# One pool of x tiles for two layers, and the last stage's first blocks in another order

## The chip, the core and the metric

The kernel runs on one core of a Trainium2 chip. A core has five engines that run side by side, each through its own list of instructions in order: TensorE (PE; its weight loads are listed apart as PEld), VectorE (DVE), ScalarE (ACT), GpSimd (POOL) and SyncE (SP), which here only issues transfers. ScalarE and GpSimd can issue transfers too. An instruction waits for semaphores that others raise, and all that is behind it on its engine waits with it. The metric is the device time of one execution in microseconds; the median of three runs of the kernel before is 3335.99 us (3325.55 to 3337.98).

## What is computed

Four layers follow one another on an image of 256 x 256 points with 128 channels. Each normalises its input over groups of four channels and the whole image, and adds its own output to it. The first two are attention along rows and a product of triangles; they are left as they are. The change lies in the third and fourth:

```python
def _L2_conv_ref(z, ...):
    zn = _layernorm(z, ln_in_w, ln_in_b)
    a = jax.nn.sigmoid(zn @ Wga + bga) * (zn @ Wla + bla)
    b = jax.nn.sigmoid(zn @ Wgb + bgb) * (zn @ Wlb + blb)
    k = jnp.einsum('bimc,bmjc->bijc', a, b)
    return jax.nn.sigmoid(zn @ Wgo + bgo) * (_layernorm(k, ...) @ Wlo + blo)

def _L3_conv_ref(x, w1, b1, w2, b2):
    t = relu(c1(x))                      # 3 x 3 taps, 128 channels to 1
    y = jnp.concatenate([x[:, :1], x[:, 1:] + t[:, :-1]], axis=1)
    u = relu(c1(y))
    z_main = u + jnp.roll(y, 1, axis=1)
    z = jnp.concatenate([z_main[:, :H - 2], u[:, H - 1:H] + y[:, H - 2:H - 1], y[:, H - 1:H]], axis=1)
    v = relu(c2(z))                      # 128 x 128 product at each point
    p = jnp.concatenate([z[:, :, :1], z[:, :, 1:] + v[:, :, :-1]], axis=2)
    r = relu(c2(p))
    q_main = r + jnp.roll(p, 1, axis=2)
    return ...                           # q_main with its last two columns put right

x = x + _L2_conv_ref(_gn(x), ...)        # gives x3
x = x + _L3_conv_ref(_gn(x), ...)        # gives the output
```

`t` and `u` are single-channel images, so the shifts by one row and one column are done on small data; their sum, one number per point called `e` below, is added to all channels.

## The kernel before

Channels lie on the 128 partitions, and the 65,536 points are cut into 32 strips of 2048 points (8 rows), 1 MB each. Between stages the data lie in DRAM: `x2T` is the input of the third layer, `x3T` of the fourth. Tiles come from pools in SBUF that are opened and closed with their stage; a pool's place is used again by the next one, and a tile's place by a later tile of the same pool, after a wait for the earlier use. In most stages the program's order is written out by hand, one list for all engines.

The third layer has three stages. **Stage 5** (L1101 to L1235) loads x2T by strips (pool `x5`, seven tiles) and makes a and b. **Stage 6** (L1260 to L1299) multiplies them channel by channel and stores k; near its end it loads the first three strips of x2T again (`load7x`, pool `x7`). **Stage 7** (L1303 to L1407), the x3 stage, goes through the strips: GpSimd spreads a row of factors (L1329), TensorE makes the gate product and the output product (L1335), VectorE scales, adds biases and multiplies (L1345, L1324, L1391), GpSimd adds the result to x in place (L1404), ScalarE sums x and its square for the next normalisation (L1349, L1350), and SP stores x to x3T (L1356) and loads the strip five ahead. For the last strip VectorE does the addition in halves (L1397) and its halves are stored apart (L1401). Seven tiles hold x, three in `x7` and four in the stage's own pool.

From the sums come mean and deviation of each group (L1414 to L1420; `r3`), and from them the tap weights `w1f` (L1424) and constants.

**Stage 9** (L1451 to L1750) is the fourth layer. Its steps, by the names used in the prediction:

- `load9` loads a strip of x3T (L1462, nine tiles).
- `taps`: TensorE makes nine tap values for each point (L1468), ScalarE copies them (L1472, into one of two buffers `p9_st`), and SP stores them to a padded image sD in DRAM (L1477, four stores a strip; strip 0 also needs the last two rows, `xe`).
- `load_block` reads the taps of 16 rows (two strips) shifted into place (L1487); VectorE sums them (`sum_taps`, L1509, L1510); ScalarE applies relu (`relu_t`, L1515); GpSimd masks the image's edge and multiplies by the taps' weights (`shift_t`, L1519, L1522); t goes to DRAM (`keep_t`, L1527) and comes back one row lower (`load_t`, L1531); VectorE sums (`image_u`, L1536), ScalarE applies relu (`relu_u`, L1540), GpSimd adds u and t (`image_e`, L1545), and e goes to DRAM (`keep_e`, L1551). This is the image chain of one block.
- `load_e` reads e back as one row for each of the two strips (L1564, 8 KB each), and `spread_e` spreads a row over the partitions on GpSimd (L1572).
- `start_z`: ScalarE normalises x into PSUM, shifted by a row (L1580). `finish_z`: VectorE adds the spread e and gives z (L1595).
- `p_half` and `q_half`: TensorE's products (L1601) with VectorE's max and add (L1609, L1623, L1626); `residual` is GpSimd's addition (L1615); L1702, L1706 and L1750 are ScalarE's small preparations of p and q; `emit` transposes (L1638), copies (L1639) and stores the output (L1640).

The tap results, the started z and the transposed outputs share two PSUM buffers.

Before the loop over strips stands a prologue (L1644 to L1694): xe and four strips are loaded, taps of strips 0 and 1 made, blocks -1 (one row) and 0 taken through the image chain, and strips 2 to 7 prepared. In the loop (L1695 to L1750) the first two passes take blocks 1 and 2 through the whole chain inside one pass; from pass 2 on the chain of a block is laid over two passes, and ScalarE issues the loads of e's rows:

```python
            if s > 3 and s % 2 == 0 and b <= NB:
                load_e(b - 1, nc.scalar)
            if s < NR:
                p_half(s, 0)
                p_half(s, 1)
                del xs[s]
            if s < 2:
                begin_image(s + 1)
            if s + 1 < NR:
                finish_z(s + 1)
            if s < 2:
                end_image(s + 1)
```

Of the kernel before, what the change touches and what calls it, by code (L numbers as in the profile page):

```python
# [9 lines left out]
F32 = mybir.dt.float32  # L10
# [22 lines left out]
def kernel(ctx: ExitStack, tc: tile.TileContext, a: dict, out: bass.AP):  # L33
# [1061 lines left out]

    rs2_scope = ExitStack()
# [4 lines left out]
    with tc.tile_pool(name="x5", bufs=7) as x5_pool, tc.tile_pool(name="p5", bufs=2) as sb, tc.tile_pool(  # L1101
# [6 lines left out]
        def load5(s):  # L1108
            if s < NSC:
                xs[s] = x5_pool.tile([P, SC], F32, name="p5_x")  # L1110
                (nc.gpsimd if s < KB else nc.sync).dma_start(xs[s], x2T[:, s * SC : (s + 1) * SC])
# [127 lines left out]
    x7_pool = rs2_scope.enter_context(tc.tile_pool(name="x7", bufs=3))  # L1239
# [15 lines left out]
    def load7x(s, pool, bufs):  # L1255
        if s < NSC:
            xs7[s] = pool.tile([P, SC], F32, name="p7_x", bufs=bufs)
            nc.sync.dma_start(xs7[s], x2T[:, s * SC : (s + 1) * SC])

    with tc.tile_pool(name="p6", bufs=3) as sb, tc.tile_pool(name="p6ps", bufs=3, space=PSUM) as ps:  # L1260
        nc.vector.memset(k1, 0.0)
        nc.gpsimd.memset(k2, 0.0)  # L1262
        with tc.manual_schedule():
# [18 lines left out]
            for c in range(D):  # L1282
# [11 lines left out]
                if c % 4 == 3:  # L1294
# [3 lines left out]
                    if q >= D // 4 - 3:  # L1298
                        load7x(q - (D // 4 - 3), x7_pool, 3)  # L1299

    g1 = const.tile([P, NSC + 1], F32, name="g1")  # L1303
    g2 = const.tile([P, NSC + 1], F32, name="g2")
    with tc.tile_pool(name="p7", bufs=2) as sb, tc.tile_pool(name="p7psX", bufs=2, space=PSUM) as psX, tc.tile_pool(
# [46 lines left out]
        def finish7(s):  # L1352
            x = xs7.pop(s)
            sums7(x, junk, s)
            del gts[s]
            nc.sync.dma_start(x3T[:, s * SC : (s + 1) * SC], x)  # L1356

        load7k(0)
        load7x(3, sb, 4)
# [13 lines left out]
        load7x(4, sb, 4)  # L1373
# [9 lines left out]
        for s in range(NSC):  # L1383
# [3 lines left out]
            for h in range(2):  # L1387
# [3 lines left out]
                nc.vector.scalar_tensor_tensor(gts[s][:, hs], pl, b2w[:, 5:6], gts[s][:, hs], ALU.add, ALU.mult)  # L1391
# [4 lines left out]
                if last:  # L1396
                    nc.vector.tensor_tensor(xs7[s][:, hs], xs7[s][:, hs], gts[s][:, hs], ALU.add)  # L1397
                    if h == 0:
                        finish7(s - 1)
                    sums7(xs7[s][:, hs], junk[:, hs], s + h)  # L1400
                    nc.sync.dma_start(x3T[:, s * SC + h * H2 : s * SC + (h + 1) * H2], xs7[s][:, hs])  # L1401
            del ks[s]
            if not last:
                nc.gpsimd.tensor_tensor(xs7[s], xs7[s], gts[s], ALU.add)  # L1404
                if s:
                    finish7(s - 1)
            load7x(s + 5, *((x7_pool, 3) if (s + 5) % 7 < 3 else (sb, 4)))  # L1407
# [36 lines left out]
    R = 8  # L1444
    NR = N // R
    H = R // 2
    BR = 16
    NB = N // BR
    BW = NP // 8
    LEAD = 6  # L1450
    with tc.tile_pool(name="p9", bufs=2) as sb, tc.tile_pool(name="p9psM", bufs=2, space=PSUM) as psM, tc.tile_pool(  # L1451
        name="p9psX", bufs=2, space=PSUM
    ) as psX, tc.manual_schedule():
        x3r = x3T.rearrange("d (h w) -> d h w", w=N)
        xs, zs, pbs, qs, blocks = {}, {}, {}, {}, {}
# [3 lines left out]
        def load9(s):  # L1459
            if s < NR:  # L1460
                xs[s] = sb.tile([P, R, N], F32, name="p9_x", bufs=9)
                nc.sync.dma_start(xs[s], x3r[:, s * R : (s + 1) * R, :])  # L1462

        def taps(x, h0, n):
# [6 lines left out]
            st = sb.tile([P, 2, N], F32, name="p9_st")  # L1471
# [3 lines left out]
            for c in range(n):  # L1475
                at = 16 + (h0 + 2 * c + 1) * NP
                nc.sync.dma_start(  # L1477
# [4 lines left out]
        def load_taps(St, row, up, width, at, lo=0):  # L1482
# [4 lines left out]
            nc.sync.dma_start(  # L1487
# [6 lines left out]
        def load_block(b):  # L1494
            St = sb.tile([P, TAPS, 2 * BW + 8], F32, name="p9_S")
            load_taps(St, b * BR, 1, BW + 8, BW)
# [436 lines left out]
```

## Time and profile before

| | us |
|---|---|
| median of three runs (range) | 3335.99 (3325.55 to 3337.98) |
| the profiled execution | 3336.53 |
| its span | 3333.7 |
| TensorE busy in the span | 3044.9 (91%) |
| VectorE | 2241.9 (67%) |
| ScalarE | 2037.7 (61%) |
| GpSimd | 1769.6 (53%) |
| mean DMA rate | 225 GB/s |
| strip loop of stage 7 and its head, from 2645 | to about 2905 |
| mean and deviation known (`r3`) | 2920.8 |
| first finished z of stage 9 begins | 2951.9 |
| last output stored, end of the span | 3333.7 |

Times in the profile count from the start of the span. A line of the timeline gives the start, the duration, the engine, the line of the program, the operation, what it writes and reads, how many were merged into the line, and in brackets how long the engine stood idle before and what ended that. "ACTq", "SPq" are the engines' instruction queues, where issued transfers show. A line of the table by stretches gives the stretch, its length, busy time and number of instructions of the five rows PE, PEld, DVE, ACT and POOL, the granted TensorE clock as a share of full speed, the mean busy share of the 16 DMA engines, and GB/s. A profile is one execution; the end of a matmul is modelled.

### The profile page before, as it was taken

The numbers are of one execution on the slowest core, as the hardware profiler recorded it, in microseconds if no ns is written. First come the engines' busy times: TensorE is split into PE (matmuls) and PEld (weight loads), VectorE is DVE, ScalarE is ACT, GpSimd is POOL, SyncE is SP. The second block draws the span as 40 slices with busy tenths as digits, with TensorE's granted clock in tenths as the row PEclk, the third lists the DMA queues.
The fourth block names the chain that finished last, engine by engine and source line by source line (L and its number), as shares of the span: only waits on it lengthen the run. The fifth ranks groups of instructions, "written<-read, shape, count | busy, mean of one in ns | idle before, by whom it ended". The sixth has DMA issues, their size and how long they took to land. (4 is left out here: it accounts for less than half of the span.)

```text
span 3333.7 us, 51741 instructions
## 1 busy us (share of the span) xinstructions
PE 3044.9 (91%) x19780; PEld 1631.0 (49%) x19780; DVE 2241.9 (67%) x2532; ACT 2037.7 (61%) x2274; POOL 1769.6 (53%) x1012
## 2 busy tenths in 40 slices
PE   5678999999999999977897999999999999839988
PEld 4525555555555555532532344444799733314444
DVE  5626888888888888873555454454455688837866
ACT  3576777777777777744476544443444477726766
POOL 4055777777777777750286000000455588727866
PEclk7799999999999999989897999999999999969999
DMA  9982333333333333349599576775899899847764
GB/s 359 355 320 93 121 108 119 109 121 111 111 120 108 117 109 122 110 172 399 170 365 403 199 309 229 281 289 190 330 351 351 325 379 385 336 149 217 228 190 134
DMA packets 295170, 749.44 MB, mean 225 GB/s; under 512 B 71399, under 2 KB 142425, under 8 KB 245737
## 3 DMA queue, kind: packets, MB, share of 16 engines
q1 hardware_dynamic: 285671, 734.83, 61.1%
q0 software_dynamic: 8544, 9.99, 0.9%
q8 instruction: 158, 2.59, 0.3%
q10 hardware_dynamic: 704, 1.26, 0.1%
q14 instruction: 93, 0.76, 0.1%
HBM read 458.34 MB, written 287.64 MB: 224 GB/s over the span
## 5 line engine op out<-in xcount | busy, mean ns | idle before, releaser
L565 DVE TENSOR_TENSOR p_e<-p_S,triT 128x1024 f32<-128x1024 f32 x512 | 609.4, 1212 | 144.3 <-PE p_S L555 144.3
L575 POOL TENSOR_TENSOR p_es<-p_e 128x1024 f32<-128x1024 f32 x256 | 603.2, 2367 | 125.8 <-issue 65.1
L573 ACT ACTIVATE p_e<-p_e,mbT 128x1024 f32<-128x1024 f32 x512 | 552.0, 1138 | 61.4 <-DVE p_e L565 61.3
L1172 PE MATMUL p_pm<-p_zn,wf 128*128 128x512 f32 x1040 | 449.0, 593 | 2.5 <-ACT p_a L1207 1.9
L540 PE MATMUL p_mm<-p_xn,w 128*128 128x512 f32 x768 | 405.3, 611 | 0.3 <-DVE p_v L535 0.3
L1172 PEld LDWEIGHTS p_pm<-p_zn,wf 128*128 128x128 f32 x1040 | 196.7, 190 | 254.8 <-issue 248.1
L555 PE MATMUL p_S<-p_q,p_k 32*128 32x256 f32 x4096 | 295.4, 400 | 3.5 <-DVE p_e L565 3.3
L1262 POOL MEMSET k<- 128x512 f32 x1 | 0.5, 520 | 506.5 <-DVE p_zn L1165 506.5
L555 PEld LDWEIGHTS p_S<-p_q,p_k 32*128 32x128 f32 x4096 | 185.9, 184 | 159.5 <-PE p_mm L531 91.7
L514 POOL TENSOR_TENSOR p_xn<-p_xn,p_rs 128x1024 f32<-128x1024 f32 x63 | 151.2, 2400 | 205.7 <-DMA p_rb<-rzD 125.9
L1891 PE MATMUL tp_z<-p_B,tp_at 128*128 128x256 f32 x1024 | 249.3, 386 | 0.7 <-DMA p_B<-bD 0.5
L588 PE MATMUL p_o<-p_e,p_v 128*32 128x256 f32 x4096 | 248.6, 383 | 0.0
L1293 POOL TENSOR_TENSOR k<-k,p_sq 128x512 f32<-128x512 f32 x128 | 163.0, 1273 | 158.1 <-ACT p_sq L1291 158.1
L1891 PEld LDWEIGHTS tp_z<-p_B,tp_at 128*128 128x128 f32 x1024 | 184.5, 190 | 22.4 <-DVE tp_at L1882 1.5
L540 PEld LDWEIGHTS p_mm<-p_xn,w 128*128 128x128 f32 x768 | 126.0, 190 | 104.6 <-issue 88.6
L588 PEld LDWEIGHTS p_o<-p_e,p_v 128*32 128x32 f32 x4096 | 120.3, 110 | 110.3 <-ACT p_g L546 41.5
L1292 DVE TENSOR_TENSOR k<-tp_z,k 128x512 f32<-128x512 f32 x128 | 88.5, 691 | 125.7 <-ACT p_sq L1291 125.7
L1615 POOL TENSOR_TENSOR p_q<-p_q,p_pb 128x2024 f32<-128x2024 f32 x32 | 144.3, 4510 | 52.4 <-ACT p_q L1706 44.0
L1289 ACT COPY p_K<-tp_z 128x512 f32<-128x512 f32 x128 | 74.9, 585 | 156.5 <-PE tp_z L1891 156.5
L546 ACT ACTIVATE p_g<-p_mm,bgh 128x512 f32<-128x512 f32 x128 | 88.0, 687 | 131.4 <-PE p_mm L540 131.3
L544 ACT ACTIVATE p_k<-p_mm,cqkg 128x512 f32<-128x512 f32 x128 | 88.0, 687 | 125.2 <-PE p_mm L540 124.9
L531 PEld LDWEIGHTS p_mm<-w,p_xn 128*128 128x128 f32 x1024 | 134.4, 191 | 61.1 <-issue 60.4
(379 smaller groups left out, 6040.5 us busy)
## 6 DMA issues: line engine op xcount, KB each, us to landing
p_x<-x2T SPq DMA_DIRECT2D x60, 1024.0 KB
x<-x1T SPq DMA_DIRECT2D x51, 1024.0 KB
p_x<-in_x_dram SPq DMA_DIRECT2D x32, 1024.0 KB
p_x<-xT SPq DMA_DIRECT2D x64, 512.0 KB
x2T<-x SPq DMA_DIRECT2D x32, 1024.0 KB
aD<-p_a SPq DMA_DIRECT2D x32, 1024.0 KB
bD<-p_b SPq DMA_DIRECT2D x32, 1024.0 KB
p_A<-aD SPq DMA_DIRECT2D x32, 1024.0 KB
```

Of the source, the lines that this page charges most:

```text
L514: nc.gpsimd.tensor_tensor(xn, xn, groups[g]["rs"], ALU.mult)
L531: nc.tensor.matmul(pm[:, k * D : (k + 1) * D], lhsT=t["xn"][:, b * P : (b + 1) * P], rhs=wf[:, 2 * D : 3 * D], start=True, stop=True,)
L540: nc.tensor.matmul(pm, lhsT=w, rhs=t["xn"][:, cs_], start=True, stop=True)
L555: nc.tensor.matmul(Ss[h // 2][:, h % 2, u, :], lhsT=t["k"][hp, r * N + u * P : r * N + (u + 1) * P], rhs=t["q"][hp, r * N : (r + 1) * N], ...
L565: nc.vector.tensor_tensor(e[:, :, 2 * p : 2 * p + 2, :].rearrange("p u h n -> p h u n"), Ss[p], triT[:, 2 * p : 2 * p + 2, :, :], ALU.add,)
L573: nc.scalar.activation(e[:, u, :, :], e[:, u, :, :], AF.Exp, bias=mbT[:, u, i : i + 1])
L575: nc.gpsimd.tensor_tensor(es, e[:, 0, :, :], e[:, 1, :, :], ALU.add)
L588: nc.tensor.matmul(t["o"][hp, r % 2, :], lhsT=t["v"][:, r * 2 + u, hp], rhs=e[:, u, h, :], start=(u == 0), stop=(u == 1),)
L1172: nc.tensor.matmul(pm[:, c, :], lhsT=wf2[:, i, :], rhs=zns[s][:, k * CK : (k + 1) * CK], start=True, stop=True)
L1293: nc.gpsimd.tensor_tensor(k2, k2, sq, ALU.add)
L1615: nc.gpsimd.tensor_tensor(q[:, :, 1 : N - 2], q[:, :, 1 : N - 2], pb[:, :, 0 : N - 3], ALU.add)
L1891: nc.tensor.matmul(pz[:, t, :], lhsT=at[:, u, t * P : (t + 1) * P], rhs=Bc[:, u, :], start=(u == 0), stop=(u == 1))
```

## The change

Five things are done.

1. The seven x tiles become one pool `x57` opened before stage 5 and closed at the end. Stages 5, 6 and 7 take their x tiles from it, and stage 9 takes seven of its nine; two more lie in its own pool.
2. In stage 7, `load7x(s + 5)` is followed, when x2T has run out (strips 27 to 31), by `load9(0)` to `load9(4)`. The last two rows `xe` are read from the last strip's tile instead of being loaded.
3. Stage 7's last two strips: GpSimd's addition for strip 30 and its sums come in halves; for strip 31 VectorE writes the scaled product back to PSUM, adds x from there, and takes the sums with four `bn_stats` and a `bn_aggr` instead of ScalarE's four passes.
4. The prologue is put into another order: taps of strips 2 and 3 are made ahead of the image chain and stored by ScalarE, which also issues the loads of block 1; the chains of blocks 0 and 1 are interleaved; strip 5 is loaded by GpSimd, whose memset also clears the first block; strips 6 and 7 are loaded at its end. `p9_st` has three buffers. The edge masks `inside` are made between stages 6 and 7. Passes 0 and 1 of the loop are now like the others.
5. `load_e` in the loop is issued by SP, right after that pass's x load, and in each even pass from 2.

```diff
+    x_scope = ExitStack()
+    x_pool = x_scope.enter_context(tc.tile_pool(name="x57", bufs=7))
...
-                xs[s] = x5_pool.tile([P, SC], F32, name="p5_x")
+                xs[s] = x_pool.tile([P, SC], F32, name="p5_x", tag="x")
...
-    def load7x(s, pool, bufs):
+    def load7x(s):
         if s < NSC:
-            xs7[s] = pool.tile([P, SC], F32, name="p7_x", bufs=bufs)
+            xs7[s] = x_pool.tile([P, SC], F32, name="p7_x", tag="x")
...
+    inside = const.tile([P, BW + 8], F32, name="inside")
+    nc.vector.memset(inside, 1.0)
...
+    def load9(s, own=None, queue=nc.sync):
+        if s < NR:
+            if s % 9 < 7:
+                xs9[s] = x_pool.tile([P, R, N], F32, name="p9_x", tag="x")
+            else:
+                xs9[s] = own.tile([P, R, N], F32, name="p9_x")
+            queue.dma_start(xs9[s], x3r[:, s * R : (s + 1) * R, :])
...
         def finish7(s):
             x = xs7.pop(s)
-            sums7(x, junk, s)
+            if s < NSC - 2:
+                sums7(x, junk, s)
+            else:
+                for h in range(2):
+                    hs = slice(h * H2, (h + 1) * H2)
+                    sums7(x[:, hs], junk[:, hs], s + h)
...
+        def stats7():
+            nc.vector.bn_aggr(mv7[:, 0:2], st7.rearrange("p n s -> p (n s)"))
+            nc.vector.tensor_tensor(mv7[:, 2:3], mv7[:, 0:1], m2, ALU.subtract)
+            nc.vector.tensor_scalar(g1[:, NSC:], mv7[:, 2:3], float(SC), None, ALU.mult)
+            nc.vector.scalar_tensor_tensor(mv7[:, 3:4], mv7[:, 2:3], mv7[:, 2:3], mv7[:, 1:2], ALU.mult, ALU.add)
+            nc.vector.tensor_scalar(g2[:, NSC:], mv7[:, 3:4], float(SC), None, ALU.mult)
...
-                nc.vector.scalar_tensor_tensor(gts[s][:, hs], pl, b2w[:, 5:6], gts[s][:, hs], ALU.add, ALU.mult)
+                nc.vector.scalar_tensor_tensor(
+                    pl if last else gts[s][:, hs], pl, b2w[:, 5:6], gts[s][:, hs], ALU.add, ALU.mult
+                )
...
                 if last:
-                    nc.vector.tensor_tensor(xs7[s][:, hs], xs7[s][:, hs], gts[s][:, hs], ALU.add)
+                    nc.vector.tensor_tensor(xs7[s][:, hs], pl, xs7[s][:, hs], ALU.add)
                     if h == 0:
                         finish7(s - 1)
-                    sums7(xs7[s][:, hs], junk[:, hs], s + h)
+                    for c in range(2):
+                        k = 2 * h + c
+                        nc.vector.bn_stats(st7[:, k, :], xs7[s][:, k * CK : (k + 1) * CK])
...
+            elif s == NSC - 2:
+                for h in range(2):
+                    hs = slice(h * H2, (h + 1) * H2)
+                    nc.gpsimd.tensor_tensor(xs7[s][:, hs], xs7[s][:, hs], gts[s][:, hs], ALU.add)
...
-            load7x(s + 5, *((x7_pool, 3) if (s + 5) % 7 < 3 else (sb, 4)))
+            load7x(s + 5) if s + 5 < NSC else load9(s + 5 - NSC)
...
-            st = sb.tile([P, 2, N], F32, name="p9_st")
+            st = sb.tile([P, 2, N], F32, name="p9_st", bufs=3)
...
-        xe = sb.tile([P, 2, N], F32, name="p9_xe", bufs=1)
-        nc.sync.dma_start(xe, x3r[:, N - 2 : N, :])
-        for s in range(4):
-            load9(s)
+        xe = xs7[NSC - 1].rearrange("p (h w) -> p h w", w=N)[:, R - 2 : R, :]
         S0 = sb.tile([P, TAPS, 2 * BW + 8], F32, name="p9_S")
-        nc.vector.memset(S0, 0.0)
+        nc.gpsimd.memset(S0, 0.0)
+        load9(5, sb, nc.gpsimd)
...
         taps(xe, N - 2, 1)
         for s in range(2):
             taps(xs[s], s * R, 4)
-        start_z(0)
         load_taps(S0, N - 1, 1, BW, BW + 4, P - 8)
         blocks[-1] = dict(St=S0)
         load_block(0)
...
+        for s in range(2, 4):
+            taps(xs[s], s * R, 4, nc.scalar)
+        for b in (-1, 0):
             sum_taps(b)
             relu_t(b)
             shift_t(b)
-            keep_t(b)
-            load_t(b)
...
+            if b < 0:
+                nc.sync.dma_start(image_rows(tD, 0, 1), blocks.pop(b)["t"][P - 8 : P, 4 : 4 + BW])
+        keep_t(0)
+        load_t(0)
+        image_u(0)
+        load_block(1, nc.scalar)
+        relu_u(0)
+        for s in range(4, 6):
             taps(xs[s], s * R, 4)
-        load_block(1)
-        for s in range(4, 8):
-            load9(s)
+        start_z(0)
+        image_e(0)
+        keep_e(0)
+        load_e(0)
+        sum_taps(1)
+        relu_t(1)
+        shift_t(1)
+        keep_t(1)
+        load_t(1)
         spread_e(0)
         finish_z(0)
+        image_u(1)
+        relu_u(1)
+        image_e(1)
+        keep_e(1)
+        load_e(1)
         spread_e(1)
+        load_block(2)
+        load9(6, sb)
+        load9(7, sb)
         for s in range(NR + 2):
             b = s // 2 + 2
-            load9(s + 8)
-            if s > 1 and s % 2 == 1 and b < NB:
+            load9(s + 8, sb)
+            if s > 1 and s % 2 == 0 and b <= NB:
+                load_e(b - 1)
+            if s % 2 == 1 and b < NB:
                 load_t(b)
...
-            if s > 3 and s % 2 == 0 and b <= NB:
-                load_e(b - 1, nc.scalar)
...
-            if s < 2:
-                begin_image(s + 1)
             if s + 1 < NR:
                 finish_z(s + 1)
-            if s < 2:
-                end_image(s + 1)
...
-            if s > 1 and s + LEAD < NR:
+            if s + LEAD < NR:
                 taps(xs[s + LEAD], (s + LEAD) * R, 4)
-            if s > 1 and s % 2 == 1 and b + 1 < NB:
+            if s % 2 == 1 and b + 1 < NB:
                 load_block(b + 1)
```

## The prediction

> **What bounds the kernel.** I read the busy shares by stage first, to see where engines are idle; then the timeline of the end of the x3 stage and the start of the last one; then the waits and timeline of the last stage's loop. The kernel takes 3336.53 us in the profiled execution, 3333.7 of it span. The table by stretches (us; busy time of each engine with its instructions; TensorE clock; DMA share; GB/s):
>
> ```profile
> 2645.00:2905.00 260.00, 254.94 (x742) 98.88 (x742) 227.10 (x188) 188.62 (x180) 206.88 (x61) 0.99 0.96 373
> 2905.00:2922.00 17.00, 3.17 (x16) 1.66 (x15) 9.32 (x21) 12.33 (x16) 3.16 (x1) 0.63 0.35 142
> 2922.00:2952.00 30.00, 5.39 (x18) 0.61 (x18) 4.13 (x9) 5.62 (x9) 4.71 (x6) 0.56 0.48 167
> 2952.00:3005.00 53.00, 30.39 (x88) 9.77 (x88) 20.93 (x23) 19.75 (x26) 19.32 (x16) 0.72 0.45 143
> 3005.00:3290.00 285.00, 264.66 (x1040) 130.46 (x1040) 219.45 (x251) 199.96 (x258) 219.56 (x172) 0.97 0.70 202
> ```
>
> The x3 stage is full (TensorE 255 of 260 us). Then come about 100 us (2905 to 3005) in which no engine is full: a serial chain. The loop after it is nearly, not quite, full. The change touches exactly these two; nothing else in it is on a path. The chain, from the timeline:
>
> ```profile
> 2905.86 3.38 DVE L1397 TENSOR_TENSOR p_x<-p_x,gate 128x1024 f32<-128x1024 f32 x1
> ...
> 2917.40 0.19 DVE L1415 TENSOR_REDUCE d<-g 128x1 f32<-128x33 f32 x1 [1.09 <-ACT p_junk L1350]
> ...
> 2933.97 0.69 ACT L1472 ACTIVATE p_st<-p_pp,s 128x512 f32<-128x512 f32 x1 [4.93 <-DMA sD<-p_st]
> ...
> 2940.55 0.81 DVE L1509 TENSOR_REDUCE p_acc<-p_S 128x41 f32<-128x369 f32 x1 [0.31 <-DMA p_S<-sD]
> ...
> 2951.85 2.36 DVE L1595 TENSOR_TENSOR p_z<-p_zp,p_eb 128x1024 f32<-128x1024 f32 x2 [8.35 <-POOL p_eb L1572]
> 2964.92 2.35 DVE L1595 TENSOR_TENSOR p_z<-p_zp,p_eb 128x1024 f32<-128x1024 f32 x2
> ```
>
> See how long it takes from the last sums (2917.4) to the first block's tap sums (2940.6) and to the first finished z (2951.9). I call the start of the VectorE add of strip s z(s): z(1) is 2964.92, z(2) 2992.23, z(3) 3004.76, and z(5) 3023.64. From there z of an even strip to the next odd one always takes 9.77 us, in which TensorE is busy all the time; odd to even takes 9.5 to 16:
>
> ```profile
> 3045.18:3059.33 14.15, 11.67 (x42) 5.38 (x40) 8.74 (x11) 9.30 (x11) 9.04 (x8) 0.88 0.86 242
> 3099.88:3109.65 9.77, 9.77 (x42) 4.79 (x40) 7.86 (x10) 7.71 (x11) 7.66 (x6) 1.00 0.52 155
> 3109.65:3120.56 10.91, 9.98 (x42) 4.79 (x40) 8.79 (x11) 7.76 (x11) 9.09 (x8) 1.00 1.04 298
> ```
>
> From z(5) to z(27) (3023.64 to 3266.56) are 11 pairs in 242.9 us, 22.08 each; at two times 9.77 they would take 214.9. So 28.0 us are lost here, and the timeline says to what:
>
> ```profile
> 3049.36 1.25 ACTq L1564 DMA_DIRECT2D p_er<-eD  x2
> 3051.13 0.69 ACT L1472 ACTIVATE p_st<-p_pp,s 128x512 f32<-128x512 f32 x1 [4.39 <-DMA p_er<-eD]
> ...
> 3112.22 1.66 ACTq L1564 DMA_DIRECT2D p_er<-eD  x2
> 3114.06 0.69 ACT L1472 ACTIVATE p_st<-p_pp,s 128x512 f32<-128x512 f32 x1 [2.84 <-PE p_pt L1638]
> ...
> 3055.38 2.30 POOL L1572 PARTITION_BROADCAST p_eb<-p_er  x1 [3.67 <-DMA p_er<-eD]
> 3116.45 2.30 POOL L1572 PARTITION_BROADCAST p_eb<-p_er  x1 [0.26 <-DMA p_er<-eD]
> ```
>
> ScalarE itself issues the loads of e's rows: it stands until the store of e has landed, and then for 1.25 to 2 us of issue; the tap copy and the output copies behind it free the PSUM buffers that TensorE needs.
>
> **The end of the x3 stage.** VectorE's first add of the last strip (3.38 us, waiting out GpSimd's add; the second took 1.23) now reads PSUM: 1.22, as L1324 took beside a busy GpSimd. The last strip's sums leave ScalarE (4.9 us, 2912.45 to 2917.37) for VectorE: four statistics at 0.685 (L648). GpSimd's add of strip 30 goes in halves and ends near 2907.1 instead of 2908.16, since its first half needn't wait for the second gate. VectorE from 2905.83: 1.22 + 1.37 + 1.28 + 1.22 + 1.37, and five small operations of 0.2, an estimate from the 0.16 to 0.22 of L1416 to L204: 2913.3, then both reductions, so L1415 starts at 2913.55. ScalarE ends its sums at 2911.65 (2902.52 + 4.2 + 4.9) and loads the square root's table in the gap. **-3.9 us.**
>
> **To the first tap sums.** After the statistics, before waits for xe (2923.69 where the weights were ready at 2921.7: 2.0), for the x strips (0.79 + 0.61), and ScalarE's third copy waits from about 2930.5 to 2933.97 for a tap buffer (3.5), whose small store lay behind 4 MB of x loads. With x and xe in SBUF and a third buffer all go: 3.9 + 2.0 + 1.4 + 3.5 = **10.8, taken as 10.5**: 2930.0 instead of 2940.55. The x loads moved up take the slots of strips already stored; the loads of x2T and k that they follow run out there, so their cover is the fading traffic of strips 27 to 31 (stores 1 MB per 5.7 us). Without cover they cost 4 MB at 420 GB/s, 9.5 us.
>
> **To z(0).** The chain t, u, e took 11.3 us. Its SP steps now stand behind eight tap stores of strips 4 and 5 (2.5 us), and relu_u behind two issues of block 1 on ScalarE (1.0); some of it lies beside the wait for t. I get 12.5: 2942.5, **-9.3**. Unknown from the trace: whether ScalarE's tap stores of strips 2 and 3 must wait for block 0's load to finish reading. If so ScalarE stands 4 us at 2926, of which 2.9 reach z(0). Ends 0 and 2.9; the nearest row, SP's tap store at 3008.62 that starts 0.75 us after its copy ended, after a block load, says rather yes.
>
> **To z(3).** Before, strips 1 and 2 each paid a whole image chain in the loop (z(1) to z(2) 27.3 us). Now block 1's chain lies beside block 0's: z(1) is 6.7 later (VectorE's two products, then GpSimd's spread 2.3), 2949.2. For z(2), block 2's row e isn't needed (block 1 holds strips 2 and 3), but ScalarE's tap copy of strip 6 stands ahead of strip 2's start, and strip 6 is only loaded after z(0), near 2949.7. Before, four such loads issued at 2961.48 gave their first strip at 2968.5, 7 us later. So taps at 2956.7, copy 2959.3, start and q 4.7, products: z(2) 2964, z(3) 2973.3. That is -28 and -31.4. From z(3) to z(5) took 18.9, and will take 19.5 to 21. With half the unknown wait and a little more, **-28 at z(5)**; ends -19 (strip 6 late by another load time, the wait in full) and -34. The masks' VectorE operations (0.9 us, 2921.8 to 2922.7) now stand ahead of the chain of k between stages: **+0.9**. The shared pool moves addresses in earlier stages; their first loads wait for stores anyway, cost 0, ends -2 and +3.
>
> **The loop.** Taking the issue from ScalarE gives at most 28.0. What is late next: the row must land before GpSimd's spread (2.3), which must end before z(even). [...]moved to SP's queue, the 8 KB rows stand behind the 1 MB x load just issued there. The row that shows it: the tap store issued at 2926.36 behind x loads landed about 2933.97, 7.6 us, where with a free queue the rows at 2947.32 were used at 2949.52. In the pair at 3109.65, SP issues block, output and x load from 3108.16 to 3112.64, 2.44 MB; 1.25 MB of it had moved by 3114 (the stretches of 1 us from 3109 sum to that), so the rest at 310 GB/s drains near 3117.8, against 3116.45 by the separate queue. [...]row at 3118, spread to 3120.3, z 10.6 after z(odd), and with t's store, 5 us in flight behind the next megabyte, pairs of 20.4 to 21.3. Without it (landing 0.9 after issue): 19.54. I take 20.7[...]: 11 times (22.08 - 20.7) = **-15**; ends 0 and -28. Behind the wait on SP stand tap stores, an output store and the next x load; none is needed within a step. The end from z(27) stays.
>
> **Sum:** -28 + 0.9 - 15 = -42. 3336.5 - 42 = 3294.5; the median of three runs, 3335.99, lies 0.5 below the profiled time: 3294.
>
> **Rivals.**
> - *The loop closes wholly* (0.20): 22 steps of 9.77; -27 - 28: 3281. For it: in the slow pairs (3172, 3220) the row already came in time for 9.77. Against: the pairs with a full DMA queue.
> - *The loop gains nothing* (0.17): rows land so late that pairs stay at 22; -27: 3309. For it: the spread waited for rows 7.6 us in six places even with a queue of their own.
> - *SP becomes the bound* (0.08): per pair SP issues 10.3 us now (x 4.9, taps 2.8, block 1.0, outputs 1.3, t 0.3), waits 5.2 for t's store (62.3 over 12), and would add 1.25 and the 3.6 of e's store: 20.3, over TensorE's 19.5. If the row then lies 9 us in flight, pairs take 24.5, which cancels the 27: the point from which it decides. At 26, 3352, slower. Against: the waits overlap work that SP has no hurry with.
> - That the early loads don't come early: their slots need the stores of strips 25 to 29, landed two steps before; the x2T loads use the same slots at that pace now.
>
> **Numbers.** My forecast 0.55 (3281 to 3307). The range 3271 to 3313 takes in the first two rivals and the cost ends, -65 to -23. A measurement tells 0.5% (16.7 us) from no change. Faster: 0.55 + 0.20 + most of 0.17 = 0.90; within: 0.06; slower: 0.04.
>
> **What will show it.** L1415's successor about 4 us earlier after the last gates; no wait of ScalarE for a tap buffer; first tap sums 10 us and z(3) 30 us earlier against the last gate; no load of p_er on ScalarE; odd to even steps near 10.5. Wrong if ScalarE stands in the prologue for its own queue, if strip 6's taps come after z(1) by more than 10 us, or if GpSimd's spread waits over 2 us in most pairs.

## The result and the profile after

The changed kernel takes **3301.8 us** (median of four runs, 3299.37 to 3308.08); the kernel before, run beside it, 3330.77 us. The ratio is 0.9915, with a 95% interval from 0.9886 to 0.9944: 29 us less. The profiled execution is the slowest of the four, 3308.08 us with a span of 3306.4; against the profiled one of before it is 28.45 us shorter (its span 27.3), and the table of places below is made between these two.

The table by stretches, cut at the same events as the one of before (columns: stretch, its length, busy us and instructions of TensorE, weight loads, VectorE, ScalarE, GpSimd; clock; DMA share; GB/s):

```profile
2656.00:2920.00 264.00, 255.34 (x741) 99.08 (x740) 227.43 (x192) 188.27 (x180) 207.80 (x61) 0.98 0.98 376
2920.00:2933.00 13.00, 3.37 (x20) 1.98 (x24) 10.51 (x25) 8.47 (x12) 3.58 (x4) 0.70 0.99 412
2933.00:2965.00 32.00, 10.24 (x53) 1.77 (x45) 5.14 (x9) 8.40 (x14) 5.82 (x9) 0.61 0.34 74
2965.00:2996.00 31.00, 21.78 (x53) 8.32 (x54) 19.32 (x21) 14.95 (x21) 19.26 (x15) 0.82 0.51 160
2996.00:3263.00 267.00, 258.16 (x1045) 128.43 (x1043) 220.16 (x250) 202.68 (x260) 219.76 (x172) 0.99 0.72 215
```

The reader is to see three things. The chain between the two full stages (rows two to four) has shrunk from 100 to 76 us. The x3 stage (first row) has grown by 4: its first products come later. The loop (last row) is shorter for the same number of strips. The timeline carries the chain and the loop. First VectorE's last add, the statistic, the tap sums of blocks -1 and 0, z(0) and z(1); then what ScalarE and GpSimd did; then two even passes of the loop:

```profile
2924.96 1.22 DVE L1438 TENSOR_TENSOR p_x<-p_pm,p_x 128x1024 f32<-128x1024 f32 x1
...
2928.65 0.19 DVE L1464 TENSOR_REDUCE d<-g 128x1 f32<-128x33 f32 x1
...
2943.31 0.80 DVE L1548 TENSOR_REDUCE p_acc<-p_S 128x41 f32<-128x369 f32 x1 [10.08 <-DMA p_S<-sD]
...
2950.43 0.81 DVE L1548 TENSOR_REDUCE p_acc<-p_S 128x41 f32<-128x369 f32 x1 [5.75 <-ACT p_t L1554]
...
2964.76 2.36 DVE L1634 TENSOR_TENSOR p_z<-p_zp,p_eb 128x1024 f32<-128x1024 f32 x2 [8.59 <-POOL p_eb L1611]
2972.68 2.35 DVE L1634 TENSOR_TENSOR p_z<-p_zp,p_eb 128x1024 f32<-128x1024 f32 x2
...
2946.28 1.59 ACTq L1516 DMA_DIRECT2D sD<-p_st  x4
2947.92 0.69 ACT L1511 ACTIVATE p_st<-p_pp,s 128x512 f32<-128x512 f32 x1 [7.26 <-DMA sD<-p_st]
2948.64 1.38 ACTq L1516 DMA_DIRECT2D sD<-p_st  x4
2950.07 0.33 ACT L1554 ACTIVATE p_t<-p_acc,b 128x41 f32<-128x41 f32 x1 [1.46 <-DMA sD<-p_st]
...
2660.02 4.49 POOL L1353 PARTITION_BROADCAST p_rb<-rs__17904  x2 [7.04 <-DVE inside L1315]
...
3098.02 2.45 SPq L1325 DMA_DIRECT2D p_x<-x3T  x1
3098.76 0.57 POOL L1590 DMA_DIRECT2D eD<-p_e  x1 [0.29 <-POOL p_e L1584]
3104.16 1.27 SPq L1603 DMA_DIRECT2D p_er<-eD  x2
3107.11 2.30 POOL L1611 PARTITION_BROADCAST p_eb<-p_er  x1 [2.21 <-DMA p_er<-eD]
...
3119.08 0.56 POOL L1590 DMA_DIRECT2D eD<-p_e  x1 [0.30 <-POOL p_e L1584]
3120.05 2.47 SPq L1325 DMA_DIRECT2D p_x<-x3T  x1
3122.61 1.27 SPq L1603 DMA_DIRECT2D p_er<-eD  x2
3128.35 2.30 POOL L1611 PARTITION_BROADCAST p_eb<-p_er  x1 [3.25 <-DMA p_er<-eD]
```

The tap sums of block -1 (2943.31) come 14.66 us after the statistic, those of block 0 only 21.78 after it. Between them lies a wait on ScalarE (`p_t`), and ScalarE's own lines say why: its tap stores stood until 2946.28. In the loop GpSimd stores e, SP waits for that store and issues the rows. In the first of the two passes the store goes out just behind the 1 MB load of x, the rows can be issued only 5.4 us later, and are spread 3 us after their issue. In the second the rows are issued 3.5 us after the store, but 2.6 us behind the load of x, and are spread 5.7 us after their issue.

What the two profiled executions give, place by place (us, changed minus before):

| place | difference | predicted |
|---|---|---|
| up to stage 4's last but one addition (1799.31, now 1804.43), code that the change leaves alone | +5.1 | 0 |
| hand-over: from there to stage 5's second reciprocal (47.8, now 52.5) | +4.7 | 0 (-2 to +3) |
| stages 5 and 6 | about +1 | 0 |
| reciprocal of k to stage 7's first addition by GpSimd | +4.5 | +0.9 |
| last gates to the statistic (12.85, now 8.77) | -4.1 | -3.9 |
| statistic to z(5) (106.24, now 86.53) | -19.7 | -24.1 |
| z(5) to z(27), 11 pairs (242.9, now 226.1) | -16.8 | -15 |
| z(27) to the end | -2.0 | 0 |

The waits of the loop (who waited for what: us in total, times, longest) show what holds it now. Before, the spread waited 7.6 us for rows in six places; TensorE's idle time, 17.9 us in ten places, all stood ahead of its output transposes, which waited for ScalarE's tap copies (first line below, from before).

```profile
PE p_pt L1638 <- ACT p_st L1472: 17.9, 10, 3.1
```

```profile
POOL p_eb L1611 <- DMA p_er<-eD: 22.0, 9, 4.2
...
DVE p_z L1634 <- POOL p_eb L1611: 13.7, 9, 3.2
PE p_pp L1507 <- DVE p_z L1634: 7.5, 6, 2.4
```

GpSimd's spread waits for the row, VectorE's z for the spread, TensorE's next products for z: one chain. TensorE idled for 8.8 of these 226.1 us, 7.5 of them here.

### The profile page after: what moved, and what is told of

Its sections match the earlier page's. It is cut to its first block, busy times and chain, and to the rows that moved or that the text cites. A ratio compares the mean times of both kernels' runs of the same rounds, so it can differ in the third digit from the quotient of the medians.

```text
span 3306.4 us, 51751 instructions
## 1 busy us (share of the span) xinstructions
PE 3040.7 (92%) x19780; PEld 1630.8 (49%) x19780; DVE 2244.1 (68%) x2540; ACT 2033.9 (62%) x2270; POOL 1773.3 (54%) x1017
## 5 line engine op out<-in xcount | busy, mean ns | idle before, releaser
L1213 DVE SCALAR_TENSOR_TENSOR p_b<-p_pm,b2w,p_b 128x1024 f32<-128x1024 f32 x64 | 82.1, 1284 | 121.3 <-PE p_pm L1174 106.9
```

## Experiments

**Theory.** The loop's gain comes from SP's issue, limited by rows that stand behind the x load on SP's queue. The three costs that were not foreseen are two places in memory and one place in a queue: the shared pool lies over stage 4's last tiles, the masks' column lies under stage 7's pool, and ScalarE's tap stores stand ahead of block -1's ReLU. **Rivals**: the loop gained from the new prologue or the third tap buffer; the rows are held by the landing of e's store and not by the queue; the differences at the stage starts are chance.

Each kernel was timed beside the kernel before. Ratios are to that kernel; a difference of medians is given only with the ratios beside it.

### Rows back to ScalarE, and rows to SP alone

In the changed kernel (`load_e` takes the queue as an argument again):

```diff
...
-            if s > 1 and s % 2 == 0 and b <= NB:
-                load_e(b - 1)
...
+            if s > 1 and s % 2 == 0 and b <= NB:
+                load_e(b - 1, nc.scalar)
```

> The changed kernel, with e's rows in the loop loaded by ScalarE again, behind q's activation, and all else as changed. Theory: the loop's 16.8 us (20.55 us for a pair of strips against 22.08) came from SP's issue alone; then a pair takes 21.9 to 22.1 us again and the kernel is 15 to 18 us slower than the changed one. Rival: the loop gained from the order that the new prologue leaves (three buffers, strips loaded further ahead); then a pair stays under 21.2 us and less than 8 us are lost.

Measured: 3327.9 us, ratio 0.9994 (0.9981 to 1.0007); the changed kernel beside it 3302.15, 0.9915 (0.9893 to 0.9937). 25.8 us are lost, more than the theory asked, and a pair takes 22.29 us: between z(5) and z(27) the profiled executions differ by 18.4 us. ScalarE in that run:

```profile
3095.16 1.99 ACT L1740 ACTIVATE p_q<-p_x,kcol 128x2048 f32<-128x2048 f32 x1
3101.02 1.25 ACTq L1603 DMA_DIRECT2D p_er<-eD  x2
3102.37 0.69 ACT L1511 ACTIVATE p_st<-p_pp,s 128x512 f32<-128x512 f32 x1 [5.23 <-issue]
```

q's activation ends at 3097.15; ScalarE then stands at the issue of the rows until 3101.02, and the tap copy starts 5.2 us after q. By the medians, everything else of the change brings nothing without the move: the whole of it is 0.9994. (The profiled execution, 3322.67, lies 5 us under its median.)

On the kernel before, the opposite edit, rows by SP and nothing else:

```diff
             load9(s + 8)
+            if s > 3 and s % 2 == 0 and b <= NB:
+                load_e(b - 1)
...
-            if s > 3 and s % 2 == 0 and b <= NB:
-                load_e(b - 1, nc.scalar)
```

> The kernel before, with e's rows in the loop loaded by SP, behind the load of strip s+8, and nothing else changed. Theory: this alone brings the loop's gain: 20.5 to 20.7 us for a pair of strips, 15 to 19 us in all. Rival: the gain needs the changed prologue; then under 8 us.

Measured: 3325.23 us, 0.9982 (0.9972 to 0.9992). The theory missed: a pair took 21.65 us, and 6 us came of 15 to 19. The rival's number is met; that a fast loop needs the changed prologue, its reason, the next runs refute. The waits of this loop:

```profile
POOL p_eb L1572 <- DMA p_er<-eD: 27.8, 7, 5.8
DVE p_z L1595 <- POOL p_eb L1572: 21.9, 8, 4.8
```

It is the changed kernel's chain again, only longer: the rows came later still. Why they come later with the old prologue isn't shown; one execution of the changed loop (21.48 in the table below) is nearly as slow.

### Rows ahead of x

On the changed kernel:

```diff
             b = s // 2 + 2
+            if s > 1 and s % 2 == 0 and b <= NB:
+                load_e(b - 1)
             load9(s + 8, sb)
-            if s > 1 and s % 2 == 0 and b <= NB:
-                load_e(b - 1)
```

> The changed kernel, with SP issuing e's rows ahead of the 1 MB load of strip s+8 in even passes. Theory: the rows land 4.5 us after their issue when they stand behind the x load on the same queue and about 2 us when they don't; what the loop still waits for is that, so a pair takes 19.6 to 20.0 us and 6 to 10 us are gained. Rival: what holds the rows is the landing of e's own store, for which SP waits in either order, and the x load now stands behind that wait; then a pair stays at 20.4 to 20.8 us, or x comes late and it is longer.

Measured: 3287.74 us, 0.9865 (0.984 to 0.9891), some 14 us better than the changed kernel and more than the 6 to 10 of the theory; the loop has 11.9 of it (214.9 us from z(5) to z(27) against 226.8 in the changed kernel's second profile). A pair takes 19.53 us, and every step between them 9.2 to 10.4. The timeline, and the loop as one stretch:

```profile
3104.70 0.56 POOL L1590 DMA_DIRECT2D eD<-p_e  x1 [0.29 <-POOL p_e L1584]
3108.43 1.28 SPq L1603 DMA_DIRECT2D p_er<-eD  x2
3109.77 0.43 SPq L1325 DMA_DIRECT2D p_x<-x3T  x1
...
3111.40 2.30 POOL L1611 PARTITION_BROADCAST p_eb<-p_er  x1
```

```profile
3007.20:3222.08 214.88, 214.88 (x882) 105.36 (x880) 183.11 (x211) 170.30 (x221) 184.37 (x144) 1.00 0.82 236
```

The rows go out first, the x load 1.3 us behind them, and the spread waits for nothing. TensorE is busy for 214.88 of 214.88 us: this loop has nothing left to wait for.

That the rows stood behind x on SP's queue isn't shown to be the whole reason. SP waits for e's store in either order (21.8 us in 12 places, against 27.1 in 7 in the changed kernel's first profile), but the store itself lands sooner. Its time from issue to landing in the loop (shortest, median, longest), in the changed kernel and with the rows ahead of x:

```profile
DMA to landing us min/median/max: 2.8/5.0/5.4
DMA to landing us min/median/max: 2.6/3.1/4.1
```

GpSimd issues this store, so it does not stand on SP's queue; yet it is late while a megabyte of x is under way. From the store's issue to the spread of its first row took 8.6 us in the median before the swap and 6.8 after it; the part up to the rows' issue fell from 5.1 to 3.0, the part behind it stayed at 3.5 and 3.6. And in the kernel before, with the rows on ScalarE's queue, those for which the spread waited and which were issued 0.8 to 2.9 us after a load of x took 4.2 to 6.0 us to be spread, against 5.3 to 6.0 on SP's queue right behind x in the changed kernel. So what the edit shows is that in this loop x must not go out just ahead of e's store and rows (a pair takes 19.53 us for 20.61). How much of it is the order on one queue, and how much the transfers that all queues have under way at once, these runs don't separate; the rival, e's store, has not fallen.

The same two lines on the kernel before, the rest of the change left out:

> The kernel before, with e's rows in the loop loaded by SP ahead of the load of strip s+8, and nothing else. The same rows behind that load gave 6 us on the kernel before and 26 us within the change. Theory: what the loop waits for is the rows standing behind 1 MB on their queue, whatever the prologue; then a pair of strips takes 19.5 to 19.9 us here too and the kernel comes to 3304 to 3309 us. Rival: the loop's gain needs the changed prologue; then a pair stays at 21.0 to 21.7 us and the time at about 3325 us.

Measured: 3305.21 us, 0.9921 (0.9897 to 0.9944), a pair 19.57 us. **One edit of the loop on the old kernel gives what the whole change gives**, and the rival that the loop needs the new prologue has fallen. The two kernels with rows ahead of x differ by the rest of the change: 17.5 us (0.9921 to 0.9865). The table of places leaves 15.6 for it (27.3 less 16.8 for the loop, plus 5.1 for the chance at the start), near enough. But it stays only where the loop doesn't lose it again.

The loops of all runs, from z(5) to z(27), each of one execution:

| kernel | rows issued by | a pair, us | spread waited for rows, us (times) | TensorE busy, us | clock |
|---|---|---|---|---|---|
| before | ScalarE | 22.08 | 7.6 (6) | 225.0 | 0.96 |
| before with shared pool | ScalarE | 20.86 | 7.2 (6) | 217.0 | 1.00 |
| the same, pool elsewhere | ScalarE | 21.54 | 8.3 (5) | 221.4 | 0.98 |
| changed, rows by ScalarE | ScalarE | 22.29 | 8.4 (6) | 225.6 | 0.96 |
| before, rows by SP | SP, behind x | 21.65 | 27.8 (7) | 221.8 | 0.97 |
| changed, masks' column moved | SP, behind x | 21.48 | 28.5 (8) | 220.2 | 0.98 |
| changed, two tiles on | SP, behind x | 20.64 | 22.1 (8) | 217.2 | 0.99 |
| changed, late taps | SP, behind x | 20.63 | 20.8 (8) | 218.4 | 0.98 |
| changed | SP, behind x | 20.55 | 22.0 (9) | 217.3 | 0.99 |
| changed, again | SP, behind x | 20.61 | 17.3 (6) | 217.1 | 0.99 |
| three edits and strip 6 early | SP, ahead | 19.83 | 13.4 (9) | 215.2 | 1.00 |
| three edits | SP, ahead | 19.65 | 9.4 (7) | 215.0 | 1.00 |
| before, rows ahead of x | SP, ahead | 19.57 | 3.3 (3) | 215.0 | 1.00 |
| changed, rows ahead of x | SP, ahead | 19.53 | 4.5 (4) | 214.9 | 1.00 |

Where SP issues, the pair goes with the wait for the rows. Where ScalarE issues, it follows the gaps of ScalarE ahead of tap copies to which the profile gives no releaser and in which the issue of the rows lies: 3.7 us in one place at 20.86, 17.6 in four at 21.54, 18.2 in four at 22.08, 26.5 in five at 22.29. The first three rows are the same loop code. A pair of before therefore has no one value: 22.08, on which the prediction was built, was the longest of three; the 20.86 comes from the fastest execution of its kernel, 3322.11 us for a median of 3334.43.

### The masks' column

```diff
-    with tc.tile_pool(name="in_col", bufs=1) as sb:
-        col = sb.tile([P, 1], F32, name="in_col")
+    col = const.tile([P, 1], F32, name="in_col")
```

> The changed kernel, with the one-column tile of the masks (in_col) placed beside the constants instead of in a pool of its own between stages 6 and 7. Theory: the start of stage 7 is 4.5 us late because its buffers lie where in_col lay, so GpSimd's first broadcast and the first load of k wait for VectorE's last mask operation, which stands behind the 3.35 us reciprocal. Then the first broadcast comes about 1 us after k's sums instead of 4.5 us after the reciprocal's end, and the kernel gains 3.5 to 4.5 us against the changed kernel. Rival: VectorE's 0.9 us of mask operations themselves, or k's late sums, hold stage 7; then the first broadcast stays where it was against the reciprocal and the time is the same within 1 us.

Measured: 3303.07 us, 0.991 (0.9889 to 0.9931), the same as the changed kernel. Yet GpSimd's first broadcast, 4.45 us after the reciprocal's start in the changed kernel (2660.02 against 2655.57), comes 1.05 after it (2648.74):

```profile
2649.79 4.49 POOL L1352 PARTITION_BROADCAST p_rb<-rs__17904  x2 [3.65 <-DMA kD<-p_K]
```

The wait for `inside` is gone, and the statistic came 267.2 us after the reciprocal instead of 273.3 in the changed kernel's second profile. So the mechanism is shown, and the time isn't: in this execution the loop had pairs of 21.48 us instead of 20.61, which is 9.6 us, and swallowed the gain.

### The shared pool

The pool alone on the kernel before, then the pool opened behind that of the gates (where stage 5's own pool began):

> The kernel before, with the pool shared by stages 5 and 7 alone (closed where stage 7 ends; the last stage keeps its own nine tiles). Theory: the shared pool brings nothing by itself and costs 4.6 us where stage 4 hands over to stage 5, so the kernel is 4 to 5 us slower than before and all later places are late by as much. Rival: the hand-over took 4.6 us more by chance; then the time is that of before within 1.5 us.

> The kernel before with the shared pool of stages 5 and 7 alone, opened after the pool of the gates, so that it begins where stage 5's own pool began. Theory: the first loads of stage 5 wait for whatever lies under any part of their pool, and the shared pool at the lower address covers the tiles that stage 4 stores last; then GpSimd's first loads stand ahead of stage 4's last addition again, and the first square of stage 5 starts about 11.5 us after that addition starts, against 21 us with the pool at the lower address. Rival: sharing itself makes the wait, wherever the pool lies; then 21 us again.

Stage 4's last addition on GpSimd and the first loads of stage 5, for the pool at the lower and then at the higher place:

```profile
1803.99 4.51 POOL L1035 TENSOR_TENSOR x<-x,p_g 128x2048 f32<-128x2048 f32 x1 [4.36 <-DVE p_g L1024]
1815.10 2.19 POOL L1113 DMA_DIRECT2D p_x<-x2T  x4 [6.60 <-DMA x2T<-x]
```

```profile
1806.30 1.68 POOL L1112 DMA_DIRECT2D p_x<-x2T  x3 [3.60 <-DMA x2T<-x]
1807.97 4.55 POOL L1035 TENSOR_TENSOR x<-x,p_g 128x2048 f32<-128x2048 f32 x1
```

At the lower place all four loads wait for the last addition and for the landing of its store (6.6 us); at the higher one three go out ahead of that addition. The first square of stage 5 starts 20.9 us after the addition's start in the one and 11.45 in the other (1824.86 and 1819.42), as the theory said. So it is the place and not the sharing. The cost is smaller than these two numbers, since the loads that go first put the addition itself off. Counted as in the table of places, from the last but one addition to stage 5's second reciprocal, it took 50.6 to 53.6 us in the ten executions with the pool at the lower place and 46.0 to 48.7 in the other four, on average 4.4 us less. The times can't tell it: 3334.43 us, 1.0005 (0.9992 to 1.0017), and 3330.34, 1.0 (0.9987 to 1.0012). One try at mending it failed. Two unused tiles, taken first, were to move strips 0 to 4 by 16 KB:

> The changed kernel, with two unused tiles taken first out of the shared pool, so that strips 0 to 4 of stage 5 lie two places (16 KB of each partition) further on, where they lay before the change. Theory: stage 5 began 4.6 us later against the end of stage 4 because the first tiles of the shared pool lie over stage 4's tiles that come free last. Then the first load of x goes out about 4.6 us earlier against stage 4 and the kernel gains 4 to 5 us against the changed kernel. Rival: the 4.6 us are the difference of two executions of the same stage; then stage 5 begins as in the changed kernel, within 1 us.

Measured: 3300.12 us, 0.9904 (0.9883 to 0.9925); GpSimd's first load came 11.1 us after the last addition's start, exactly as without them. That it is the pool's place as a whole which waits, and not each tile's, fits both runs; the profile shows no addresses, so this stays an inference.

### The changed kernel again

> The changed kernel once more, on the chip of the three runs above, as their yardstick. If the 5 us by which its profiled execution lay behind by the end of stage 3, whose code the change does not touch, are chance, this execution shows stage 3 ending within 3 us of the kernel before; if the change's placement caused them, again 4 to 6 us.

Measured: 3302.15 us. Its last but one addition of stage 4 starts at 1797.71, 1.6 us ahead of before's (1799.31), where the first profile had 1804.43. The +5.1 of the table is chance.

### The tap stores of strips 2 and 3

```diff
-        for s in range(2, 4):
-            taps(xs[s], s * R, 4, nc.scalar)
         for b in (-1, 0):
             sum_taps(b)
             relu_t(b)
...
+        for s in range(2, 4):
+            taps(xs[s], s * R, 4, nc.scalar)
         keep_t(0)
```

> The changed kernel, with the tap products of strips 2 and 3, whose stores ScalarE issues, written behind the ReLUs of blocks -1 and 0. Theory: block 0's tap sums wait for the ReLU of block -1 (one accumulator), and that stands on ScalarE behind the store of strip 2's taps, which waits on its queue until 2946.3. Then block 0's sums start about 5 us earlier, z(0) comes 2 to 5 us earlier, and as strip 6's x holds z(2), 0 to 2 us of it stay in the time. Rival: the stores don't matter and the sums wait for the rows; then block 0's sums start where they did, within 1 us.

Measured: 3300.22 us, 0.9901 (0.9879 to 0.9924). Block 0's sums follow those of block -1 by 1.66 us instead of 6.6 (the changed kernel's second profile), as the theory said. But z(0) comes 35.6 us after the statistic, against 35.05 there: nothing is gained. ScalarE and VectorE show where it went:

```profile
2941.13 0.81 DVE L1548 TENSOR_REDUCE p_acc<-p_S 128x41 f32<-128x369 f32 x1 [0.28 <-DMA p_S<-sD]
...
2943.57 0.50 DVE L1575 TENSOR_REDUCE p_u<-p_prod 128x33 f32<-128x330 f32 x1 [0.99 <-POOL p_prod L1561]
...
2942.90 1.59 ACTq L1516 DMA_DIRECT2D sD<-p_st  x4
2945.32 1.38 ACTq L1516 DMA_DIRECT2D sD<-p_st  x4
2948.07 1.06 ACTq L1526 DMA_DIRECT2D p_S<-sD  x2
2949.17 0.32 ACT L1579 ACTIVATE p_u<-p_u,b 128x33 f32<-128x33 f32 x1 [3.89 <-issue]
```

The sum `p_u` is there at 2944.07, and its ReLU waits until 2949.17 behind the stores and behind block 1's load, which waits for them to land. The same 5 us have moved from one ReLU to the next on ScalarE.

### The mended version, and strip 6 earlier

Rows ahead of x, the column beside the constants and the late taps together:

> The changed kernel with e's rows ahead of x (as in the run that came to 3287.7 us), the masks' column beside the constants, and the tap products of strips 2 and 3 behind the ReLUs of blocks -1 and 0. Theory: with the rows in time the loop runs at TensorE's pace, 9.8 us a strip, and no longer swallows what the stages ahead of it gain; then the 4.5 us at the start of stage 7 and up to 2 us of the prologue stay, and the time is 3281 to 3284 us. Rival: the loop gives them back, as it did when the masks' column alone was moved (a pair took 21.5 us for 20.6); then the time is 3286 to 3290 us.

Measured: **3281.81 us, 0.9853 (0.9827 to 0.988)**, the lowest median of all kernels here and in the theory's band. But its interval lies largely over that of rows ahead of x alone, and the profiled execution (3286.27) is only 2.4 us shorter than the other's (3288.66): the statistic came 3.5 us earlier against the reciprocal, the prologue and the loop lost 1.1 and 1.2 of it. How much of the gain at stage 7's start stays is open.

With strip 6's load on ScalarE's queue right behind the products of z(0):

> The same three edits, and strip 6's x loaded by ScalarE's queue as soon as the products that start z(0) have read its place, instead of by SP at the end of the prologue. Theory: z(2) comes 14 us after z(1) because strip 6's taps wait for that load; then z(2) follows z(1) by 9.8 to 11 us and 3 to 4.5 us are gained over the run with three edits. Rival: block 1's row or the tap sums of block 2 hold z(2) as long; then z(2) follows by 13 to 14 us and nothing is gained.

Measured: 3282.57 us, 0.985 (0.9824 to 0.9877). TensorE's tap product of strip 6, here and then in the run with three edits:

```profile
2963.27 1.78 PE L1506 MATMUL p_pp<-p_x,w1f 128*32 128x512 f32 x8 [2.55 <-issue]
```

```profile
2966.69 1.94 PE L1506 MATMUL p_pp<-p_x,w1f 128*32 128x512 f32 x8 [5.83 <-DMA p_x<-x3T]
```

The load's wait is gone and z(2) follows z(1) by 8.9 us instead of 12.3, so the theory of the place holds. The time doesn't move: the loop's pairs took 19.83 us instead of 19.65, with the spread waiting 13.4 us for rows instead of 9.4. By z(5) the edit had gained 3.3 us in these two executions, and the loop lost 2.0 of them again; why its rows came later isn't shown.

## Why the prediction came out as it did

The forecast of 3294 us was 8 us too low, within its own range, and its direction and its two main sources hold. As a gain it was further off: 29 us of the 42 forecast, since the kernel before, run beside the changed one, took 3330.77 and not 3336. Between the two profiled executions the missing part is the chance at the start (5.1), the two places in memory (4.7 and 3.6) and the prologue (4.4); the loop and the end gave 3.8 more than forecast. Two of its own signs of being wrong came: ScalarE stood in the prologue at its own tap stores, and GpSimd's spread waited over 2 us in 6 of the 11 pairs. Step by step:

- **The end of the x3 stage, -3.9**: -4.1. VectorE's add from PSUM took 1.22, as taken from the like row, and so it did beside GpSimd's add (at 2921.19, GpSimd's from 2917.78 to 2922.48), where before's add from SBUF, begun beside GpSimd's, took 3.38. The square root's table load, 1.28 us from 2927.09, ended 2.95 us ahead of its use; statistics and sums as added up.
- **To the first tap sums, -10.5**: the part that rests on loads and on the third buffer holds. (The 420 GB/s of its estimate is the rate of before's four loads at 2961.48: 401 to 442 GB/s in each microsecond from 2965 to 2975.) Block -1's sums stand 14.66 us after the statistic, and ScalarE no longer stands for a buffer ahead of the copies that they need. Block 0's sums are where it failed.
- **To z(0), -9.3: the term that failed.** The text asked whether ScalarE's tap stores must wait for block 0's load, said "rather yes", and gave it 2.9 us at most. The answer is yes. z(0) came 7.2 us later than forecast (36.1 after the statistic for 28.95): 5.3 of this stand already at block 0's tap sums (21.8 for 16.45), 1.8 come behind them. The estimate counted one stand of ScalarE beside other work. It didn't count that the ReLU of block -1 stands behind both stores, and block 0's sums behind that ReLU through the one accumulator. The late taps show the 5 us to be ScalarE's queue: they reappear at the next ReLU.
- **To z(5), -28**: -23.8, inside the ends of -19 and -34. Strip 6's load landed 6.8 us after its issue and held z(2), as written; from z(0) on the steps went 2.7 us better than taken.
- **Masks +0.9 and shared pool 0**: both were priced as work, and both cost a wait at a place in memory: +4.5 (the 0.9 of work in it) and +4.7, the second outside its ends. The column and the pool's place, moved one at a time, took these waits away.
- **The loop, 20.7 for a pair**: 20.55. The number was met, in part by luck. That the rows would be held behind x on SP's queue was the author's assumption, from one row of before (a tap store that landed 7.6 us after its issue behind x loads). By the estimate from it a pair was to take 20.4 to 21.3, and with rows that land 0.9 us after their issue 19.54. With the rows behind x it took 20.55 to 20.64 in four executions and 21.48 in a fifth, on the kernel before 21.65; with the rows ahead 19.53. The numbers fit the two estimates, but e's store on GpSimd's queue was held up beside x as well (5.0 us to its landing, 3.1 with the rows ahead), so the order on SP's queue isn't shown to be the cause. What the step did not see is that its base of 22.08 was one execution of a loop that took 20.9 to 22.1: on the kernel before, the move alone was worth 6 us, not 15.
- **The rivals.** "The loop closes wholly" was wrong for the change and right for one edit more; "the loop gains nothing" and "SP becomes the bound" have fallen: with SP issuing the rows, and ahead of x, TensorE was busy without a gap.

Open: why the new prologue with ScalarE's rows makes a slower loop than the old one with them (22.29 us for a pair against 20.86 to 22.08), so that together they gain nothing. The profile shows ScalarE standing longer at the rows; what shifts the two against each other wasn't separated, nor was the third tap buffer tried alone. Open too is what of the loop's gain is the order on SP's queue and what the earlier landing of e's store.

## What to carry to other kernels

When small transfers that something waits for go out beside a large load that nothing waits for yet, issue the large one last: the rows moved to SP and ahead of x were alone worth as much here as the whole change (0.9921 and 0.9915). Price a move by what comes to stand behind the moved instruction on its engine (here 5 us at ScalarE's tap stores) and by whose memory its tile takes over (4.5 and 4.7 us), not by its duration. And where the loop behind an edit waits for transfers, time saved ahead of it can vanish there, as the 6.1 us won ahead of it with the masks' column moved did in 9.6 us of longer pairs: close the loop first, and read its base from more than one execution.

## What the hardware showed unexpectedly

TensorE's stalls cost more than their length in this loop. The 882 matmuls of the loop are the same in all kernels; before, as one stretch:

```profile
3023.64:3266.56 242.92, 224.96 (x882) 109.74 (x880) 182.88 (x211) 170.29 (x221) 184.22 (x144) 0.96 0.73 209
```

TensorE idled 18 us, and was busy for 225 us at a granted clock of 0.96; with the rows ahead of x it idled for none and was busy for 214.9 at 1.00. So of the 28 us between the two loops 10 were TensorE's own pace. The clock in the loop of before was granted in full or by half (1.00 or 0.50). The first two gaps of TensorE with a halved stretch behind them, each gap followed by its stretch:

```profile
3049.40:3051.88 2.48, 0.01 (x1) 0.01 (x1) 2.05 (x4) 0.75 (x2) 2.30 (x3) 1.00 1.06 259
3052.85:3056.26 3.41, 3.41 (x7) 1.35 (x6) 0.00 (x0) 3.22 (x7) 0.89 (x1) 0.50 0.39 152
3176.36:3179.29 2.93, 0.00 (x1) 0.00 (x1) 2.05 (x4) 0.74 (x2) 2.30 (x3) 0.98 0.72 296
3179.15:3182.56 3.41, 3.27 (x10) 2.44 (x11) 0.00 (x0) 2.25 (x5) 2.30 (x1) 0.50 0.13 24
```

Four gaps, of 2.48, 2.93, 2.80 and 3.09 us, each had such a stretch begin within 1 us of its end, 17.1 us of them in all; the six shorter ones, of 0.59 to 1.78, had none. At half the clock these 17.1 us cost up to 8.5 us of work (an estimate, half of 17.1), most of the 10. What sets off a halved stretch isn't shown. The length of the gap alone doesn't tell: in the changed kernel's loop a gap of 2.39 us had no halving behind it, and the only halved stretch, 3.41 us at 0.50, began 1.3 us after a gap of 1.71. The prediction's target of 9.77 us a strip had all this in it unseen, since it was read from steps without a stall.
